# Reordered transfers, ScalarE copies and block transposes in a four-layer graph network on one Trainium2 core

## The chip, the core and the metric

The kernel runs on one core of a Trainium2 chip. A core has five engines that run side by side and meet only at semaphores: TensorE (matrix products, here PE), VectorE (DVE), ScalarE (ACT), GpSimd (POOL) and SyncE (SP). DMAs are issued from SP, ACT and POOL and are carried by 16 DMA engines that all queues share. The metric is the device time of one execution in microseconds (us), the median of several runs.

## What is computed

A graph of 3327 nodes with 512 features each goes through four layers. Every layer adds its result to its input and normalizes each row. Layers 0, 2 and 3 are graph attention with 8, 8 and 4 heads; layer 1 averages over up to 64 neighbours.

```python
def attention(h, adj, W, a):                      # layers 0 (no elu), 2 and 3
    Wh = h @ W                                    # by head
    e = leaky_relu(s1[:, None] + s2[None, :], 0.2)   # s1, s2: Wh times the two halves of a
    att = softmax(where(adj > 0, e, -9e15), axis=-1)
    return elu(att @ Wh)

def layer1(X, A):
    keep = (A > 0) & (cumsum(A, axis=1) <= 64)
    cnt = keep.sum(axis=1)
    xj = leaky_relu((keep @ X / max(cnt, 1)) @ W_nb.T + b_nb)
    return leaky_relu(X @ W_line.T + b_line) + where(cnt > 0, xj, 0)

x = layernorm(x + layer(x))                       # four times
```

## The kernel before

**Tiles and halves.** Nodes are cut into 26 tiles of 128 (`NT`), and these into two halves of 13 (`HALF`). The mask of edges stays in SBUF as 8-bit floats. An attention layer runs in eight units: for each half of the target nodes, four slices `s` of 128 features. With 8 heads a slice holds two heads (`HS == 2`, layers 0 and 2), with 4 heads one (`HS == 1`, layer 3).

**A unit** (`unit`, L361) loops over the 26 source tiles `j`. For each head, VectorE makes the weights `t` (L402) from a row broadcast `rb`, a column `qc` and the mask; ScalarE makes from `t` an 8-bit step `y` (L405); TensorE multiplies `t` with the values `vj` into `po` (L425). Two tiles later `den` (L377) adds the softmax denominators into `pd`, from `y` and from the small matrices `sden` and `sm`. These hold each source's factors, cut into three bf16 pieces whose sum is the factor, by `cut` (L321). For half 0 of the sources `cut` runs before the layer's loop, for half 1 as a job within its first unit.

**After a unit** `po` is copied to `ob` by ScalarE and VectorE, TensorE transposes it (L453), ScalarE copies the result to `hb` (L457; two buffers, `sp` pool) and SP stores it to the DRAM array `hd`. In layer 3, for half 0, the path is another (`by_dma`): VectorE transposes blocks of 32x32 straight out of `po` (L443) and four DMAs per unit place them in `hd` (L465). For half 1 of layer 3 (`final`) TensorE's transposes are taken into an SBUF array `g` instead of `hd` (L951 for the first two slices).

**Denominators.** When a half is done (in layer 3, half 1, after slice 1 and after slices 2 and 3) VectorE transposes `pd` into `db` (L486, L487) and sums the pieces into `red` (L491); SP writes these to a DRAM array `dd` in four DMAs (L495) and reads them back as `pes` (L498); `finish_sums` (L501) makes the reciprocals `rec`. For the very last slice TensorE does this with a product against `c1w` (L533).

**Order of work.** TensorE runs in the order of the program text. The other engines' orders are set by a scheduler from a model of the times, except where `keep_in_program_order` holds an instruction in its place. A job list spreads side work, one job for each source tile: `nothing` is an empty job. Each engine takes its instructions in that order, so one that waits holds back those behind it.

**Between the layers.** After layer 0, `finish` (L202) loads rows of `hd` and of the input (`xr`), divides by the denominators, adds and normalizes, two tiles at a time; the first two tiles are finished as `ending` of the last unit. Layer 1 (`sage`, L645) first projects each tile (L690, L693) into a value split in three bf16 parts, two kept in SBUF (`zs`) and one sent through DRAM (`zd`, read back as `zl`). Then, for each of 26 output tiles, TensorE adds 26 x 3 products into `acc` (L809). The kept edges `kt` (L774) are made beforehand by a running count in `pk`, which starts from carries `cy` that POOL loads for four source tiles at a time. `cb` and `cnt` (L740 to L745) are the neighbour counts of every node, `wsb` the weights of layer 2's projection, `bnb` a bias. Layer 2 is followed by `third` (L836), which finishes layer 2's tiles and projects them for layer 3.

## Time and profile before

| what | us |
|---|---|
| runs | 3405.98, 3407.31, 3412.4 |
| median | 3407.31 |
| profiled execution | 3407.9, span 3406.2 |

The span runs from the first to the last instruction that the profiler recorded. How it is shared out by stage, in us from its start:

| stretch | what runs |
|---|---|
| 0 to 145 | load of the mask, projection of layer 0 |
| 145 to 953 | attention of layer 0, with neighbour counts and the rest of the mask as jobs |
| 953 to 1005 | passage from layer 0 to layer 1 |
| 1005 to 1165 | layer 1, projections |
| 1165 to 1207 | layer 1, first output tile |
| 1207 to 1754 | layer 1, other output tiles, with layer 2's projection |
| 1754 to 1778 | passage to layer 2 |
| 1778 to 2556 | attention of layer 2 |
| 2556 to 2706 | passage and projection for layer 3 |
| 2706 to 3373 | attention of layer 3 |
| 3373 to 3406 | last slice, normalization and output |

Groups of instructions that the change touches, from the page and from the list of groups (count, busy us, mean ns of one):

| line, engine | what | count | busy | mean |
|---|---|---|---|---|
| L402 DVE | `t`, 128x1664 | 1040 | 1959.9 | 1957 |
| L405 ACT | `y`, 128x1664 | 1040 | 1771.1 | 1766 |
| L453 PE | transposes of `ob` | 260 | 44.7 | 290 |
| L486, L487 DVE | transposes of `pd` | 28 | 17.1 | 637, 586 |
| L491 DVE | sums of pieces | 14 | 6.9 | 530 |
| L348 DVE | `sm` from pieces | 20 | 6.8 | 380 |
| L629 DVE | counts to bf16, 128x512 | 6 | 4.1 | 683 |
| L635 DVE | `nb`, 128x512 | 6 | 4.1 | 681 |
| L951 DVE | `g` from PSUM, 128x512 | 6 | 4.1 | 683 |
| L533 PE | sums by product, last slice | 26 records | 3.1 | 257 |

A busy time is the union of a group's records, so groups of two engines may lie over each other. DMA issues on SP are not counted as busy: a slow issue shows only in the chain of waits and in SP's own order of instructions. Several short VectorE instructions in a row overlap by part of their length, so the distance between two starts is what one of them costs.

### The profile page before, as it was taken

How to read it: one execution, taken by the hardware profiler on the slowest of the kernel's cores; microseconds unless marked ns; L12 is line 12 of the kernel's file. 1: busy time of each engine (PE TensorE's matmuls, PEld its weight loads, DVE VectorE, ACT ScalarE, POOL GpSimd, SP SyncE). 2: the span in 40 equal slices, each digit the busy share in tenths (PEclk: the TensorE clock that was granted, in tenths of full speed). 3: DMA queues.
4: the chain of work that ended last, by engine and by line, in shares of the span. 5: the costliest groups of instructions: out<-in, count | busy, mean ns of one | idle time of the engine just before them, and what ended most of it. 6: DMA issues, size and time to landing. Idle time of an engine off the chain costs nothing.

```text
span 3406.2 us, 47019 instructions
## 1 busy us (share of the span) xinstructions
PE 3262.8 (96%) x18423; PEld 1631.0 (48%) x18423; DVE 2695.3 (79%) x2630; ACT 2351.4 (69%) x2128; POOL 214.7 (6%) x344
## 2 busy tenths in 40 slices
...
GB/s 372 214 127 123 52 49 53 42 49 28 38 123 128 116 111 87 90 85 85 85 81 26 41 50 48 56 44 47 35 25 225 169 41 42 41 51 79 95 42 48
DMA packets 313365, 284.65 MB, mean 84 GB/s; under 512 B 134253, under 2 KB 248631, under 8 KB 313144
## 3 DMA queue, kind: packets, MB, share of 16 engines
...
q8 instruction: 145, 2.38, 0.3%
...
## 4 chain that ended last, share of the span: by engine, by line
PE 79%; issue 7%; DVE 6%; DMA 4%; ACT 2%; POOL 0%; SPq 0%; ACTq 0%; POOLq 0%; DVEq 0%
PE po L425 49%; PE acc L809 9%; PE pd L377 7%; PE pw L268 5%; DVE t L402 4%; PE pz L690 3%; PE pi L693 3%; DMA raw<-in_adjT_dram 2%; ACT y L405 1%; PE pt L453 1%; DMA cy<-ctd 1%; PE pk L770 1%; PE pt L258 0%; PE pa L1022 0%; DVE mask L593 0%
## 5 line engine op out<-in xcount | busy, mean ns | idle before, releaser
L402 DVE SCALAR_TENSOR_TENSOR t<-rb,qc,mask 128x1664 f32<-128x1664 f32 x1040 | 1959.9, 1957 | 167.7 <-PE po L425 150.1
L405 ACT ACTIVATE y<-t,bi,sc 128x1664 fp8e4<-128x1664 f32 x1040 | 1771.1, 1766 | 317.3 <-PE pd L377 304.4
L425 PE MATMUL po<-t,vj 128*64 128x448 f32 (+3 forms) x8320 | 1924.6, 520 | 25.0 <-DVE t L402 22.3
L425 PEld LDWEIGHTS po<-t,vj 128*64 128x64 f32 (+1 forms) x8320 | 848.3, 148 | 978.2 <-issue 689.7
L809 PE MATMUL acc<-zs,kt 128*128 128x512 bf16 x1352 | 405.1, 382 | 0.0
L809 PEld LDWEIGHTS <-kt 128*128 128x128 fp8e4 x2028 | 199.1, 98 | 250.8 <-issue 9.5
L268 PE MATMUL pw<-wsb,xT 128*128 128x264 f32 (+1 forms) x1248 | 299.8, 395 | 9.2 <-DVE vt L274 7.5
L762 ACT CAST pk<-cy 128x512 f32<-128x512 bf16 x169 | 98.9, 587 | 294.5 <-DVE kt L774 251.1
L377 PE MATMUL pd<-y,sden 128*32 128x448 fp8e4 (+1 forms) x4160 | 259.4, 342 | 8.2 <-ACT y L405 8.2
L268 PEld LDWEIGHTS pw<-wsb,xT 128*128 128x128 f32 x1248 | 240.4, 196 | 53.4 <-issue 5.0
L809 PE MATMUL acc<-zl,kt 128*128 128x512 bf16 x676 | 257.8, 381 | 4.0 <-DMA zl<-zd 4.0
L774 DVE SCALAR_TENSOR_TENSOR kt<-pk,mask 128x512 fp8e4<-128x512 f32 x169 | 116.0, 687 | 99.7 <-PE pk L770 99.7
L377 PEld LDWEIGHTS <-sden 128*32 128x32 bf16 x4160 | 117.6, 96 | 160.3 <-issue 137.6
L274 DVE TENSOR_TENSOR vt<-pw,dc 128x256 f32<-128x256 f32 x156 | 59.0, 418 | 141.2 <-ACT dc L269 137.1
L356 POOL DMA_DIRECT2D rb<-r x40 | 21.9, 548 | 1617.0 <-DVE t L402 1604.5
L272 ACT COPY rc<-pw 128x8 f32<-128x8 f32 (+1 forms) x78 | 12.7, 163 | 138.7 <-PE pw L268 136.2
L690 PE MATMUL pz<-wn,xT 128*128 128x512 f32 x208 | 97.4, 613 | 10.1 <-ACT xT L684 10.1
L693 PE MATMUL pi<-wl,xT 128*128 128x512 f32 x208 | 93.5, 592 | 0.0
L659 POOL DMA_DIRECT2D cy<-ctd x91 | 67.9, 746 | 338.4 <-ACT pk L762 310.2
L782 DVE SCALAR_TENSOR_TENSOR y<-acc,cnt,bnb 128x512 f32<-128x512 f32 x26 | 19.5, 751 | 85.9 <-PE acc L809 85.9
L593 DVE TENSOR_SCALAR mask<-raw 128x832 fp8e4<-128x832 int32 (+2 forms) x90 | 53.1, 598 | 40.4 <-DMA raw<-in_adjT_dram 40.1
L154 ACT ACT_TABLE_LOAD x45 | 57.7, 1283 | 37.3 <-DVE mv L153 36.7
...
## 6 DMA issues: line engine op xcount, KB each, us to landing
...
```

What stands on the lines that cost most here:

```text
L268: nc.tensor.matmul(pw[e][:, :FW + H], xT[:, c, :], wsb[:, c, e, :], start=c == 0, stop=c == FC - 1)
L274: nc.vector.tensor_tensor(vt[:, hs, :], pw[e][:, :FW].rearrange("p (h d) -> p h d", d=D), self.dc[:, t, hs].rearrange("p (h e) -> p h e", e=1)
L377: nc.tensor.matmul(pd[c][32 * kk:32 * kk + 32, :w_], lhsT, rhs, start=(kk, c) not in seen, skip_group_check=final is not None, stop=last a ...
L402: nc.vector.scalar_tensor_tensor(t, rb[k], self.qc[:, j, h:h + 1], mask[:, j, i0:i0 + IW], op0=ALU.max, op1=ALU.mult)
L405: nc.scalar.activation(y, t, AF.Sigmoid, bias=self.bi[:, j, h:h + 1], scale=self.sc[:, j, h:h + 1], saturate=False)
L425: nc.tensor.matmul(po[c][k * D:(k + 1) * D, :z - a_], vj[:, j % 2, k * D:(k + 1) * D], ts[k][:, a_:z], start=j == 0, stop=j == NT - 1)
L659: nc.gpsimd.dma_start(out=cy[:, :n, :], in_=ctd[t:t + n, b * GW:(b + 1) * GW] .rearrange("(o t) i -> o t i", o=1).to_broadcast([P, n, GW]))
L690: nc.tensor.matmul(pz, xT[:, c, :], wn[:, c, :], start=c == 0, stop=c == FC - 1)
L693: nc.tensor.matmul(pi, xT[:, c, :], wl[:, c, :], start=c == 0, stop=c == FC - 1)
L762: nc.scalar.copy(pks[k % 2], carry[b, t // 4 * 4][:, t % 4:t % 4 + 2, :])
L774: nc.vector.scalar_tensor_tensor(kt, pk, NEIGHBOURS, mask[:, t:t + 2, i0:i0 + GW], op0=ALU.is_le, op1=ALU.mult, saturate=False)
L809: nc.tensor.matmul(acc, kts[t][:, s * P:(s + 1) * P], zs(t, c) if c < 2 else zl[:, t, :], start=t == 0 and c == 0, stop=t == NT - 1 and c ...
```

## The change

It has six parts.

1. `cut`: the six casts to bf16 pieces and the multiplications into `sm` run on ScalarE instead of VectorE.
2. `count_jobs`: the counts' cast runs on ScalarE, and `nb` is made from `ct` in SBUF instead of from `pn` in PSUM.
3. Denominators: for half 0 of layers 0 and 2 they are summed by TensorE (`by_pe`), with `pd` copied by ScalarE. Elsewhere, `dd` keeps the layout of `red`, is written with one DMA and read back by sixteen (`place`), on POOL, or on SP at the end of a layer (`end`), and there as the last job but one.
4. `finish` as `ending`: the two `xr` tiles lie in the two `hb` buffers, and in layer 2 `e` has two buffers.
5. Layer 1: `cb` and `cnt` move ahead of the projections; for the first output tile the `zl` products come after all others; `wsb` is loaded by SP after that tile instead of by POOL before it.
6. Layer 3, half 1, slices 0 and 1: block transposes and DMAs to `hd` as in half 0, and one DMA that reads `hd` back into `g` some jobs later.

The diff, cut to its core:

```diff
@@ -162,7 +162,7 @@
-    def finish_steps(pool, xin, layer, t0, n, hbufs=6, eng=nc.sync, xbufs=None):
+    def finish_steps(pool, xin, layer, t0, n, hbufs=6, eng=nc.sync, xbufs=None, xpool=None, ebufs=None):
         H, D = layer.H, layer.D
@@ -171,7 +171,8 @@
                 ys.append(h)
-                xr = pool.tile([P, F], F32, name="xr", bufs=xbufs)
+                xr = xpool.tile([P, F], F32, name="xr", tag="hb") if xpool else \
+                    pool.tile([P, F], F32, name="xr", bufs=xbufs)
                 load_tile(xr, xin, t, nc.gpsimd)
@@ -181,7 +182,7 @@
             if layer.elu:
-                e = pool.tile([P, F], F32, name="e")
+                e = pool.tile([P, F], F32, name="e", bufs=ebufs)
                 nc.scalar.activation(e, h, AF.Exp)
@@ -329,13 +330,13 @@
                     nc.vector.tensor_tensor(dc, dc, qc, op=ALU.mult)
-                ins = nc.vector.tensor_copy(pc[:, :, :, c0], dc)
+                ins = nc.scalar.copy(pc[:, :, :, c0], dc)
                 if pinned:
...
                 nc.vector.tensor_tensor(rest, dc, pc[:, :, :, c0], op=ALU.subtract)
-                nc.vector.tensor_copy(pc[:, :, :, c0 + 1], rest)
+                nc.scalar.copy(pc[:, :, :, c0 + 1], rest)
                 nc.vector.tensor_tensor(rest, rest, pc[:, :, :, c0 + 1], op=ALU.subtract)
-                nc.vector.tensor_copy(pc[:, :, :, c0 + 2], rest)
+                nc.scalar.copy(pc[:, :, :, c0 + 2], rest)
             HS = self.HS
@@ -345,8 +346,7 @@
                 for c0, f in ((0, -0.5), (3, -1.0)):
-                    nc.vector.tensor_scalar(m[:, :, :, c0:c0 + 3], pc[:, :, k::HS, c0:c0 + 3], f, None,
-                                            op0=ALU.mult)
+                    nc.scalar.mul(m[:, :, :, c0:c0 + 3], pc[:, :, k::HS, c0:c0 + 3], f)
@@ -432,11 +432,11 @@
             if ending:
-                ending()
+                ending(sp)
             den(NT - 2, late)
             ob = sp.tile([P, IW], F32, name="ob", bufs=1)
-            by_dma = HS == 1 and not final
+            by_dma = HS == 1 and not (final and s > 1)
             for c, (a_, z) in enumerate(CUTS):
@@ -465,6 +465,8 @@
                                       in_=ob[32 * b:32 * b + 32, :].rearrange("p (q f) -> p q f", f=32))
+                if final:
+                    jobs += [nothing] * 3 + [lambda: final(s, 0, HALF, None)]
             else:
@@ -479,7 +481,9 @@
                 nc.gpsimd.memset(db[64:, WB:], 0.0)
-            if not (final and s == NS - 1):
+            by_pe = HS == 2 and half == 0 or final and s == NS - 1
+            if not by_pe:
@@ -489,14 +493,20 @@
                     nc.vector.tensor_reduce(red[:, :, o, :], dv[:, :, :, 3 * o:3 * o + 3], AX.X, ALU.add)
-                dd = dram.tile([IW, 2, 2 * NS], F32, name=f"dd{self.li}{half}{s}")
-                for kk in range(4):
-                    i_, w_ = (0, WA) if kk < 2 else (WA, WB)
-                    nc.sync.dma_start(out=dd[i_:i_ + w_, kk % 2, :].rearrange("(b i) x -> i b x", i=32),
-                                      in_=red[32 * kk:32 * kk + 32, :w_ // 32].rearrange("p b o s -> p b (o s)"))
+                dd = dram.tile([P, WA // 32, 2 * NS], F32, name=f"dd{self.li}{half}{s}")
+                nc.sync.dma_start(out=dd, in_=red.rearrange("p b o s -> p b (o s)"))
                 pes = sp.tile([P, HALF, 2, 2, NS], F32, name="pes", tag="red", bufs=1)
-                nc.sync.dma_start(out=pes.rearrange("p q k o s -> p q (k o s)"),
-                                  in_=dd.rearrange("(q p) k x -> p q (k x)", p=P))
+                end = half == 1 and s == NS - 1
+                def place():
+                    for kk in range(4):
+                        q0, nq = (0, NA) if kk < 2 else (NA, HALF - NA)
+                        src = dd[32 * kk:32 * kk + 32, :4 * nq].rearrange("i (q m) x -> m i q x", m=4)
+                        for m in range(4):
+                            ins = (nc.sync if end else nc.gpsimd).dma_start(
+                                out=pes[32 * m:32 * m + 32, q0:q0 + nq, kk % 2].rearrange("p q o s -> p q (o s)"), in_=src[m])
+                            if end and kk + m == 0:
+                                tc.keep_in_program_order(ins)
@@ -512,33 +522,42 @@
-                jobs += [nothing] * max(0, 6 - len(jobs))
-                at = 6 if half == 0 or s < NS - 1 else len(jobs)
+                if end:
+                    return jobs + [place, finish_sums]
                 if final and s > 1:
-                    return [nothing] * 5 + [finish_sums] + jobs[2:]
-                return jobs[:at] + [finish_sums] + jobs[at:]
+                    return [nothing, nothing, place, nothing, nothing, nothing, finish_sums] + jobs[2:]
+                jobs += [nothing] * max(0, 7 - len(jobs))
+                return jobs[:2] + [place] + jobs[2:7] + [finish_sums] + jobs[7:]
...
                 nc.scalar.copy(db[:64, c * (WA // 2):(c + 1) * (WA // 2)], pd[c][:64, :WA // 2])
-                nc.vector.tensor_copy(db[64:, c * (WB // 2):(c + 1) * (WB // 2)], pd[c][64:, :WB // 2])
+                (nc.scalar.copy if HS == 2 else nc.vector.tensor_copy)(
+                    db[64:, c * (WB // 2):(c + 1) * (WB // 2)], pd[c][64:, :WB // 2])
             held = []
...
-                pe = po[0][:, :2 * HALF * H].rearrange("p (q o h) -> p q o h", q=HALF, o=2)
+                pe = po[0][:, :2 * HALF * H].rearrange("p (q o h) -> p q o h", q=HALF, o=2) if final else \
+                    qp.tile([P, HALF, 2, H], F32, name="pe", tag="q")
                 held.append(pe)
...
                     e = int(q >= NA)
-                    nc.tensor.matmul(pe[:, q, :, :], db[:, (q - e * NA) * P:(q - e * NA + 1) * P], c1w[:, :, e, :],
+                    cc = c1[:, :, 8 * e:8 * e + 8] if HS == 2 else c1w[:, :, e, :]
+                    nc.tensor.matmul(pe[:, q, :, :], db[:, (q - e * NA) * P:(q - e * NA + 1) * P], cc,
                                      start=True, stop=True)
             def reciprocals():
-                pe = held[0]
-                nc.vector.tensor_tensor(r_[:, :, 0, ss], pe[:, :, 0, ss], rc[:, :, 0, ss], op=ALU.mult)
-                nc.vector.tensor_tensor(r_[:, :, 0, ss], pe[:, :, 1, ss], r_[:, :, 0, ss], op=ALU.add)
+                pv = held[0].rearrange("p t o (k s) -> p t o k s", k=HS)
+                for k in range(HS):
+                    ins = nc.vector.tensor_tensor(r_[:, :, k, ss], pv[:, :, 0, k, ss], rc[:, :, k, ss], op=ALU.mult)
+                    if HS == 2:
+                        tc.keep_in_program_order(ins)
+                    nc.vector.tensor_tensor(r_[:, :, k, ss], pv[:, :, 1, k, ss], r_[:, :, k, ss], op=ALU.add)
                 nc.vector.reciprocal(rec[:, t0:t0 + HALF, hs], rec[:, t0:t0 + HALF, hs])
+            if not final:
+                return jobs[:2] + [sums, nothing, reciprocals] + jobs[2:]
@@ -626,13 +645,13 @@
                 ct = pool.tile([P, 4 * P], BF, name="ct", bufs=1)
-                nc.vector.tensor_copy(ct[:, :w_], held["p"][:, :w_])
+                nc.scalar.copy(ct[:, :w_], held["p"][:, :w_])
                 pn = qp.tile([P, 4 * P], F32, name="pn", tag="q")
...
                 nb = pool.tile([P, 4 * P], F8, name="nb", bufs=1)
-                nc.vector.tensor_scalar(nb[:, :w_], pn[:, :w_], 0.0, None, op0=ALU.is_equal, saturate=False)
+                nc.vector.tensor_scalar(nb[:, :w_], ct[:, :w_], 0.0, None, op0=ALU.is_equal, saturate=False)
                 nc.sync.dma_start(out=mask[P - 1:P, NT - 1, i0:i0 + w_], in_=nb[NT:NT + 1, :w_])
@@ -704,6 +723,14 @@
+                cb = zp.tile([P, NT], BF, name="cb")
+                nc.gpsimd.dma_start(out=cb, in_=ctd[NT:NT + 1, :].rearrange("o (t p) -> p (o t)", p=P))
+                cnt = zp.tile([P, 3, NT], F32, name="cnt")
+                nc.vector.tensor_scalar(cnt[:, 0, :], cb, NEIGHBOURS, 1.0, op0=ALU.min, op1=ALU.max)
+                nc.vector.reciprocal(cnt[:, 1, :], cnt[:, 0, :])
+                nc.vector.tensor_scalar(cnt[:, 2, :], cb, 0.0, None, op0=ALU.is_gt)
                 pend = None
@@ -727,8 +754,6 @@
                 wsb = wp.tile([P, FC, 2, FW + nxt.H], F32, name="wsb")
-                load_wide(wsb, wsrc, nc.gpsimd)
-                nc.vector.tensor_copy(wsb[:, :, :, FW:], wa[nxt.li].rearrange("p c (e h) -> p c e h", e=2))
@@ -736,13 +761,6 @@
                 nc.gpsimd.dma_start(out=bnb, in_=bn.to_broadcast([P, F]))
-                cb = wp.tile([P, NT], BF, name="cb")
-                nc.gpsimd.dma_start(out=cb, in_=ctd[NT:NT + 1, :].rearrange("o (t p) -> p (o t)", p=P))
-                cnt = wp.tile([P, 3, NT], F32, name="cnt")
-                nc.vector.tensor_scalar(cnt[:, 0, :], cb, NEIGHBOURS, 1.0, op0=ALU.min, op1=ALU.max)
-                nc.vector.reciprocal(cnt[:, 1, :], cnt[:, 0, :])
-                nc.vector.tensor_scalar(cnt[:, 2, :], cb, 0.0, None, op0=ALU.is_gt)
@@ -805,7 +823,8 @@
                                 kts += kept(0, len(kts))
-                            for c in range(3):
+                            for c in range(2 if t0 + s == 0 else 3):
                                 nc.tensor.matmul(acc, kts[t][:, s * P:(s + 1) * P],
@@ -815,6 +834,11 @@
                                 jobs.pop(0)()
+                        if t0 + s == 0:
+                            for t in range(NT):
+                                nc.tensor.matmul(acc, kts[t][:, :P], zl[:, t, :], start=False, stop=t == NT - 1)
+                            load_wide(wsb, wsrc, nc.sync)
+                            nc.vector.tensor_copy(wsb[:, :, :, FW:], wa[nxt.li].rearrange("p c (e h) -> p c e h", e=2))
                         y = output(acc, t0 + s)
@@ -948,7 +972,8 @@
                     if s < 2:
-                        nc.vector.tensor_copy(g[:, qs, s * P:(s + 1) * P], pt[:, :n])
+                        nc.gpsimd.dma_start(out=g[:, qs, s * P:(s + 1) * P], in_=hd[HALF * P:, s * P:(s + 1) * P]
+                                            .rearrange("(q p) f -> p q f", p=P))
                         return
@@ -1072,7 +1097,7 @@
         L0.attention(rp, first_jobs, mask_steps(rawp, pieces, 1, [k for k in range(len(pieces)) if k % 5 in (1, 3)], True),
-                     ending=lambda: ends.extend(finish(f0, x, L0, 0, 2, 2)))
+                     ending=lambda sp: ends.extend(finish(f0, x, L0, 0, 2, 2, nc.sync, None, sp)))
@@ -1088,7 +1113,7 @@
                              if (half, s) == (0, 0) else [],
-                             ending=lambda: ends.extend(finish(f2, x2, L2, 0, 2, 2)))
+                             ending=lambda sp: ends.extend(finish(f2, x2, L2, 0, 2, 2, nc.sync, None, sp, 2)))
             third(ends)
```

## The prediction

> **What bounds the kernel now.** I read three views in this order: the page's busy shares, busy time by stage, and the chain of waits inside two passages between stages. First the page:
>
> ```profile
> PE 3262.8 (96%) x18423; PEld 1631.0 (48%) x18423; DVE 2695.3 (79%) x2630; ACT 2351.4 (69%) x2128; POOL 214.7 (6%) x344
> ```
>
> TensorE looks like the bound at 96%. The stages say otherwise. In the next view the columns are the stretch and its length, then busy us of PE, PEld, DVE, ACT and POOL, the granted clock, the DMA share and GB/s:
>
> ```profile
> 145.00:952.90 807.90, 787.78 (x5724) 340.49 (x5726) 805.62 (x494) 736.18 (x490) 7.66 (x15) 0.99 0.20 60
> 952.90:1005.00 52.10, 36.48 (x153) 17.93 (x150) 29.31 (x65) 21.68 (x34) 9.46 (x16) 0.84 0.57 169
> 1165.00:1207.50 42.50, 32.60 (x111) 13.21 (x110) 14.73 (x25) 9.89 (x17) 10.10 (x13) 0.84 0.66 176
> 1778.50:2556.00 777.50, 768.41 (x5440) 348.29 (x5442) 777.39 (x444) 722.42 (x476) 7.07 (x14) 0.99 0.13 41
> 2556.00:2598.00 42.00, 22.31 (x136) 16.39 (x133) 26.72 (x58) 23.93 (x39) 11.85 (x19) 0.76 0.72 219
> 2706.00:3373.00 667.00, 664.07 (x2735) 333.37 (x2734) 488.25 (x416) 459.80 (x327) 17.28 (x31) 1.00 0.20 55
> ```
>
> The reader is to see three kinds of stage. In the attention of layers 0 and 2 (rows one and four) VectorE is busy 805.6 of 807.9 us and 777.4 of 777.5 us: it is the bound, and TensorE waits inside its rows. In layer 3 (last row) TensorE is the bound, 664 of 667 us. Rows two, three and five are passages: no engine is full, the clock is 0.76 to 0.84, the DMA share is 0.57 to 0.72. Here a chain of transfers decides. The chain of waits gives, for the passage after layer 0 and for the one inside layer 1 (start us, us, what):
>
> ```profile
> 964.56 6.68 SPq L495
> 971.30 3.01 SPq L495
> 974.35 2.84 DMA dd<-red
> 977.25 2.52 DMA pes<-dd
> 979.80 0.23 DVE rec L507
> ...
> 1179.26 11.53 DMA cb<-ctd
> 1190.81 0.18 DVE cnt L743
> 1191.26 0.64 DVE kt L774
> ```
>
> The first is the denominators' trip through DRAM, held up at the issue (L495) by full DMA engines. The second is a tiny load of counts, `cb`, for which VectorE waits in order, while `kt`, which feeds TensorE, stands behind it.
>
> **What the Trainium skill says.** "DMA: Bandwidth & Descriptors", section "Queues, rings and completion order": each DMA engine takes turns between the queues it has work for, packet by packet. The trace agrees that SP's small stores share the engines with POOL's loads: `hd<-hb` issued at 962.18 us frees its buffer for ScalarE only at 974.30, and an L495 issue that takes 0.54 us in mid-layer takes 6.68 here. "TensorE: Matmul & The Clock Gate", Part 1: an idle window of about 3.4 us puts the array back to half clock. The trace agrees: after 10.06 us idle, eight L690 records take 6.38 us, later 3.60. "VectorE: DVE Perf Modes", "Why PSUM operands drop a tier": SBUF sources allow faster modes than PSUM. No run here shows it for this operation. "ScalarE: Activation LUTs", "What ACT_TABLE_LOAD costs", is used below for a price.
>
> **The change part by part.** The sum is made against the profiled span, 3406.2 us; the median of the other runs is 3407.3, 1.1 above.
>
> Layers 0 and 2, in the loop. VectorE's cost of an operation is taken from start to start, since short ones overlap (a 0.40 us cast at 158.48 is followed by the next start 0.13 later).
> - Pieces to ScalarE: per cut, six casts (L332, L336, L338) and four multiplies (L348). Inside the loop of layer 0 they advance VectorE by 0.24 + 0.24 + 0.52 + 0.96 = 1.96 us, of layer 2 by 1.94. ScalarE gets six copies at 186 + 0.833 x 104 = 273 ns and four at 316 ns by the skill's price, an estimate of 2.9 us, within its 72 us idle in row one and 55 us in row four. The added wait: each subtraction (L335, L337) now waits for a ScalarE copy queued among sigmoids of 1.77 us, and the `t` operations behind it on VectorE, so TensorE, wait with it. Between 0 (other `t` are ordered in between) and 4.7 us each (ScalarE's longest such wait for `pd`). I take 0, as VectorE has six `t` buffers.
> - Half-0 denominators: four transposes 2.46, two reduces 0.90, four products 0.48 and a reciprocal 0.71 = 4.55 us leave VectorE; four products 0.48 and a reciprocal 0.71 come back. Saved 3.35 us a layer. TensorE gets 13 products, 26 records, 3.07 us by the same group in the tail (L533). Four copies of `pd` go to ScalarE, 4 x 0.5 = 2 us. The four dd writes and one read-back vanish here.
> - Counts (layer 0 alone): eight casts L629, 4.05 us, move to ScalarE (8 x 0.57, from the 128x512 copy L457). L635, 3.98 us in all, reads SBUF instead of PSUM: 0 to 3 saved, I take 2. The wait added: the product L631 stands in TensorE's order 2.4 us behind its cast, and may now wait up to one sigmoid, 1.77 us.
>
> So VectorE loses 1.96 + 3.35 + 4.05 + 2 = 11.4 us in layer 0 and 1.94 + 3.35 = 5.3 in layer 2. TensorE is close behind: 16 products take 3.01 us when they do not wait, plus 0.87 / 2 of `pd`, 3.44 us per source tile against 3.73 paced by VectorE. After the other products about 4 us a unit of room is left, so the lead is used up slowly. I take 70%: **-8.0 and -3.7 us**; bounds 0 and the whole.
>
> Layer 3, first two heads of half 1. Four groups of transposes (0.60 + 0.60 + 0.66 + 0.33 = 2.19 us) leave TensorE twice: 4.4 us where it is the bound. VectorE swaps a 0.61 copy and 2.3 of L951 copies for four block transposes, 2.10 us, within its idle time. ScalarE loses six copies. Eight L465 stores on SP (4.6 us for four) lie between prefetched `vj` loads, as after half 0, where TensorE shows no gap; two read-backs and three sets of sixteen small loads go to POOL, busy 17 of 667 us. Against it, VectorE's transposes must free `po` in time: 0 to 2 us. **-4**, from -8 (the 1.78 us wait and slow clock at 3209 go too) to +1.
>
> Passage inside layer 1. `cb` and its three operations move ahead of the first loop, `wsb` (1 MB) behind the first output tile, and that tile's `zl` products to its end. Now the first tile runs 1176 to 1207.4, 31 us; at full rate it needs 78 x 0.216 + 13 x 0.216 = 19.7. What remains is carries `cy`: five loads, two buffers, each some 4 to 5 us to land while `zl` streams, bring the last pair to about 1194; then its products and 26 x 0.216 = 5.6 us of `zl` end near 1200. **-7** (-10 to -3). `wsb` is needed some 25 us later and hidden; its two issues stand behind the `zl` loads on SP.
>
> Passage to layer 2. The cut of half 0 shares VectorE with the first `t`: from 1769.29 to 1772.77 it holds them back 3.5 us, and TensorE's 2.39 us wait at 1778.5 is for such a `t`. Half of the cut goes: **-1.5** (-3 to +2, if copies queue behind L292's 2.98 us DMA wait).
>
> Passage after layer 2. The second `xr` load, now with its own buffer, no longer waits for the first sum (issued at 2562.98, landed 2566.2), nor `e`; TensorE's first gap, 10.61 us, shrinks, but the second, 8.85 us, waits for tiles behind `rec`. The path to `rec`: one dd write (instead of 8.1 us of L495), the last `hd` store at about 2570.1, then sixteen small reads on SP. SP's issues here cost 0.33 to 0.67; at 0.5 that is 8 us, landing 1.9 later: 2580.5 against 2583.3. **-3** (-10 to +3).
>
> Passage after layer 0. The same, but here the last `hd` stores wait for ScalarE, 976.0. Then 8 us of issues and 1.9: `rec` at 986 instead of 979.8. The four `h` loads on SP (977.7) wait behind them too. `cb` on POOL (1.49 us to issue, some 3 us of crawling DMA at 1187) comes between `blb` and the `h` loads. The paired `xr` saves VectorE 2.29 us that are not on the path. **+5** (-6, if tiles 2 and 3 go ahead of `rec`, to +10).
>
> Sum: -8.0 - 3.7 - 4 - 7 - 1.5 - 3 + 5 = -22.2 us, 0.65%: 3407.3 - 22.2 = **3385 us**.
>
> **The rivals.**
> - A, all of it lands: VectorE's whole 16.7, layer 3 -8, passages -10, -3, -10, -6: -54, 3354 us. For it: VectorE has no idle time. Against: TensorE is 2% behind.
> - B, the passages give it back: the sixteen pieces issue at 1 us each, as L495 does when engines are full. Passage after layer 0 +13, after layer 2 +5, the rest as forecast: -24.2 + 18 = -6, 3401 us.
> - C, slower: VectorE waits for ScalarE at each piece. Twelve handovers in two in-loop cuts at 4.7 us are +56, less the -22: 3441 us. It decides once a handover costs over 22.2 / 12 = 1.9 us, about one sigmoid. For it: ScalarE is 91% busy and takes its queue in order. Against: many `t` can stand between the subtractions.
>
> That the change is not what runs is excluded: each part changes instructions.
>
> **How the numbers follow.** Forecast 0.52 (3372 to 3396), A 0.16, B 0.20 (3396 to 3407), C 0.12. A measurement of this kernel tells 0.2%, 6.8 us, from no change. Faster than 3400.5: 0.52 + 0.16 + 0.13 of B = 0.81; within: 0.07 of B and 0.02 of C = 0.09; slower: 0.10. The range 3360 to 3405 leaves out part of A, a little of B and C.
>
> **What would show it.** Right: no VectorE wait on `cb` near 1190, the first output tile near 22 us, layers 0 and 2 shorter by some 8 and 4 us at VectorE 100%, layer 3 shorter by 4. Wrong: VectorE idle before L335 or L337, TensorE idle before L631, `rec` after layer 0 later than 990, or a layer 3 no shorter.

## The result, and the profile after

| kernel | median us | runs | lowest to highest | ratio to before, 95% interval |
|---|---|---|---|---|
| before | 3406.99 | 4 | 3405.98 to 3412.4 | |
| changed | 3421.33 | 4 | 3418.32 to 3425.04 | 1.0039 (1.0022 to 1.0057) |
| changed, again beside later runs | 3420.81 | 10 | 3415.31 to 3423.4 | 1.0030 (1.0020 to 1.0039) |

The change makes the kernel slower by 0.3 to 0.4%, 11 to 14 us. The forecast was 22 us faster, and 3421 lies outside its range of 3360 to 3405. The profiled execution has a span of 3420.7 us against 3406.2 before.

The page of the changed kernel, busy time of each engine:

```profile
PE 3258.0 (95%) x18397; PEld 1625.6 (48%) x18449; DVE 2671.0 (78%) x2552; ACT 2377.1 (69%) x2196; POOL 242.4 (7%) x392
```

VectorE did lose 24 us of work (2695.3 before), and ScalarE took on 26. Read alone, this line says that the change did what it was made for. The stages say otherwise. Below are busy times by stretch of the changed kernel, with the same columns as in the prediction; the stretches answer to its six rows in order of time, and the seventh row is the first of layer 0's eight units:

```profile
149.10:957.20 808.10, 785.89 (x5750) 336.31 (x5752) 795.03 (x470) 743.59 (x512) 8.98 (x17) 0.99 0.20 60
957.20:1016.00 58.80, 34.75 (x153) 18.09 (x149) 30.06 (x68) 24.54 (x37) 9.64 (x15) 0.80 0.52 144
1186.80:1218.00 31.20, 23.85 (x89) 9.73 (x90) 7.80 (x12) 6.43 (x12) 5.77 (x8) 0.84 0.79 223
1786.00:2566.00 780.00, 768.08 (x5470) 347.54 (x5472) 776.92 (x435) 733.17 (x494) 9.15 (x18) 0.99 0.13 41
2566.00:2610.00 44.00, 27.88 (x159) 20.52 (x156) 30.81 (x70) 28.11 (x44) 12.39 (x20) 0.81 0.67 219
2714.00:3387.00 673.00, 664.03 (x2709) 331.32 (x2708) 484.68 (x406) 459.77 (x329) 47.65 (x81) 0.99 0.22 60
149.10:274.10 125.00, 111.69 (x811) 45.96 (x811) 114.63 (x88) 106.90 (x86) 1.12 (x2) 0.93 0.37 110
```

In layer 0's loop VectorE is now idle for 13 us of 808 (2.3 us of 807.9 before), and 10.4 of these lie in the first unit alone (last row: 114.63 busy of 125.00). In layer 3 TensorE, the bound there, is idle for 9 us where it was idle for 3, and POOL is busy 48 us instead of 17.

To see where the time went, I cut both spans at TensorE's products: the first and last `po` product of each layer, the start of each of its eight units, the first `pz` of the third projected tile (the first that needs `rec`), and the first `acc` product of output tiles one and two.

| stage, us | before | changed | changed again | forecast | measured, first profile |
|---|---|---|---|---|---|
| start to first `po` | 145.0 | 149.1 | 149.0 | not counted | +4.1 |
| layer 0, units 1 to 8 | 811.6 | 811.8 | 808.5 | -8.0 | +0.2 |
| of it: unit 1 | 120.0 | 125.0 | 121.8 | | +5.0 |
| unit 3 (counts) | 102.4 | 99.8 | 99.8 | | -2.6 |
| unit 5 (denominators) | 100.8 | 97.9 | 97.9 | | -2.9 |
| passage after layer 0 | 41.0 | 47.6 | 49.0 | +5 | +6.6 |
| layer 1, first output tile | 31.3 | 31.2 | 30.5 | -7 | -0.1 |
| passage to layer 2 | 21.3 | 22.2 | 22.8 | -1.5 | +0.9 |
| layer 2, units 1 to 8 | 784.8 | 783.4 | 783.6 | -3.7 | -1.4 |
| of it: unit 1 | 105.0 | 107.1 | 107.4 | | +2.1 |
| unit 5 (denominators) | 101.4 | 98.0 | 98.0 | | -3.4 |
| passage after layer 2 | 146.0 | 144.3 | 145.0 | -3 | -1.7 |
| layer 3, units 1 to 8 | 669.1 | 675.0 | 674.7 | -4 | +5.9 |
| of it: units 6, 7, 8 | 84.8, 84.3, 81.4 | 82.7, 90.9, 82.8 | 82.7, 90.6, 82.8 | | -2.1, +6.6, +1.4 |

The measured column sums to +14.5, the difference of the spans; the stages left out moved by 0.5 or less. The rows of whole layers are sums of the eight rounded units. Most units whose work is the same repeat to 0.1 us from profile to profile. Some stages don't: the start and layer 0's first unit, where VectorE waits for the mask's loads, the passages after layers 0 and 2, and unit 5 of layer 0, which took 97.9, 98.9 or 100.5 in kernels with the same part 3. Kernels that run the same instructions there differ by 2 to 7 us, so only larger differences, or ones that several kernels show, are read from them.

Part of this spread goes with TensorE's granted clock (the third number from the end of a row). Unit 5 of layer 0 in the changed kernel and in two of the kernels below:

```profile
575.68:673.55 97.87, 96.88 (x729) 43.04 (x727) 97.37 (x57) 92.55 (x65) 1.26 (x3) 1.00 0.16 50
```

```profile
562.66:661.50 98.84, 97.85 (x729) 44.07 (x727) 97.62 (x57) 92.55 (x65) 1.26 (x3) 0.98 0.16 50
```

```profile
567.03:667.54 100.51, 99.52 (x730) 44.76 (x728) 97.65 (x57) 92.55 (x65) 1.26 (x3) 0.97 0.15 49
```

VectorE's and ScalarE's work is the same to 0.3 us, and the unit is longer as the clock is lower: 97.9 at 1.00, 98.8 to 98.9 at 0.98, 100.5 at 0.97 in all kernels with part 3. Where two units are compared below, the clock of both matters.

Four places in the trace of the changed kernel carry the rest. The first is before layer 0's loop, in order of time (start, us, engine, line, what; in brackets the idle time before it and what ended it):

```profile
85.09 0.82 ACT L333 CAST pc<-dc 128x104 bf16<-128x104 f32 x1
85.42 1.39 ACT L312 COPY rr<-pr 8x512 f32<-8x512 f32 x2
86.39 1.23 PE L310 MATMUL pr<-ident,rc 128*8 128x128 f32 x5 [5.37 <-ACT rr L312]
```

`rr`, which empties the PSUM bank that TensorE's next transposes need, now stands behind the casts of `pc` in ScalarE's order, and these wait for VectorE's subtractions. TensorE waits 5.37 us; before, 0.51.

The second is layer 0's first unit:

```profile
173.60 1.95 DVE L402 SCALAR_TENSOR_TENSOR t<-rb,qc,mask 128x1664 f32<-128x1664 f32 x1 [3.44 <-PE po L425]
...
176.46 0.24 ACT L312 COPY rr<-pr 8x128 f32<-8x128 f32 x1
...
176.61 0.66 ACT L333 CAST pc<-dc 128x104 bf16<-128x104 f32 x1
...
186.42 0.55 ACT L648 CAST ct<-pct 128x512 bf16<-128x512 f32 x1
...
187.03 0.58 PE L650 MATMUL pn<-ct,below 128*128 128x512 bf16 x1 [3.53 <-ACT ct L648]
...
193.44 1.95 DVE L402 SCALAR_TENSOR_TENSOR t<-rb,qc,mask 128x1664 f32<-128x1664 f32 x1 [3.08 <-PE po L425]
```

The first cast of `cut` comes at 176.61, right behind the last of four `rr` copies, two of which wait for the transfer of the one before. Counted from the layer's first product that is 14 us later than in the kernel before, where it ran on VectorE (at 158.48). There the cut filled VectorE's time up to 170; now VectorE makes six `t` in a row, has no free buffer left and is idle for 3.44 us. The cut comes when it is short of time again, and meets the counts: their cast `ct` queues behind the pieces and the sigmoids, TensorE waits 3.53 us for it, and VectorE runs out of free buffers once more (3.08).

The third is the passage after layer 0, from the chain of waits:

```profile
968.42 10.94 DMA hd<-hb
979.45 0.54 ACT hb L457
...
981.07 0.61 SPq L506
...
981.74 5.85 DMA pes<-dd
...
988.47 1.65 DMA pes<-dd
...
990.25 0.21 DVE rec L517
990.46 0.60 DVE st L152
...
991.52 0.57 ACT xT L703
992.13 5.26 PE pz L709 x8
```

`rec` is there at 990.25, which is 29.5 us after the layer's last product (960.8); before, 23.3. The sixteen reads are issued only from 981.07 on, since SP takes its queue in order and the second pair of `hd` stores stands ahead of them. The chain goes on behind `rec`: VectorE has the statistics `st` of the next pair there, a root on ScalarE waits for these, and ScalarE's copy `xT` of the first tile stands behind that root, although this tile needs no `rec`. TensorE's first projection starts 31.3 us after the layer's last product, 19.1 before. From `rec` on the passage then takes 18.2 us, 17.7 before, so nearly all of the 6.6 us lies ahead of `rec`.

The fourth is the end of unit 7 in layer 3:

```profile
3300.60 1.28 ACT L962 ACT_TABLE_LOAD   x1
3301.89 0.42 ACT L962 ACTIVATE e<-g 128x256 f32<-128x256 f32 x1
3302.32 1.28 ACT L405 ACT_TABLE_LOAD   x1
3303.62 1.77 ACT L405 ACTIVATE y<-t,bi,sc 128x1664 fp8e4<-128x1664 f32 x1
...
3305.44 0.91 PE L377 MATMUL pd<-y,sden 128*32 128x448 fp8e4 x6 [4.46 <-ACT y L405]
```

An exponential for `g` with its two table loads, 3 us in all, stands in front of the unit's last sigmoid. The unit can't end without that one, and TensorE waits 4.46 us.

### The profile page after: what moved, and what is told of

The parts are those of the page before. It is cut to its first block, busy times and chain, and to the rows that moved or that the text cites. A ratio compares the mean times of both kernels' runs of the same rounds, so it can differ in the third digit from the quotient of the medians.

```text
span 3420.7 us, 47075 instructions
## 1 busy us (share of the span) xinstructions
PE 3258.0 (95%) x18397; PEld 1625.6 (48%) x18449; DVE 2671.0 (78%) x2552; ACT 2377.1 (69%) x2196; POOL 242.4 (7%) x392
## 4 chain that ended last, share of the span: by engine, by line
PE 80%; issue 6%; DMA 5%; ACT 4%; DVE 4%; POOL 1%; SPq 0%; ACTq 0%; POOLq 0%; DVEq 0%
PE po L425 49%; PE acc L828 10%; PE pd L377 7%; PE pw L269 5%; DVE t L402 3%; PE pz L709 3%; PE pi L712 3%; DMA raw<-in_adjT_dram 2%; ACT y L405 2%; DMA cy<-ctd 1%; PE pt L453 1%; PE pk L788 1%; DMA hd<-hb 0%; PE pa L1047 0%; PE pt L259 0%
## 5 line engine op out<-in xcount | busy, mean ns | idle before, releaser
L425 PEld LDWEIGHTS po<-t,vj 128*64 128x64 f32 (+1 forms) x8320 | 838.4, 148 | 986.1 <-issue 708.9
L828 PE MATMUL acc<-zs,kt 128*128 128x512 bf16 x1312 | 394.5, 382 | 2.2 <-issue 0.2
L828 PE MATMUL acc<-zl,kt 128*128 128x512 bf16 x638 | 241.8, 379 | 0.6
L356 POOL DMA_DIRECT2D rb<-r x40 | 21.3, 532 | 1692.9 <-DVE t L402 1667.8
```

The source lines that it names most:

```text
L425: nc.tensor.matmul(po[c][k * D:(k + 1) * D, :z - a_], vj[:, j % 2, k * D:(k + 1) * D], ts[k][:, a_:z], start=j == 0, stop=j == NT - 1)
L828: nc.tensor.matmul(acc, kts[t][:, s * P:(s + 1) * P], zs(t, c) if c < 2 else zl[:, t, :], start=t == 0 and c == 0, stop=t == NT - 1 and c ...
```

## The experiments

Stages of all kernels that ran, in us (profiled execution), then span, median of all runs and ratio. u is a unit, p0, p1 and p2 are the passages after layer 0, to layer 2 and after layer 2, o1 the first output tile.

| kernel | start | L0 u1 | L0 u3 | L0 u5 | p0 | o1 | p1 | L2 u1 | p2 | L3 u6 | u7 | u8 | span | median | ratio (95%) |
|---|---|---|---|---|---|---|---|---|---|---|---|---|---|---|---|
| before | 145.0 | 120.0 | 102.4 | 100.8 | 41.0 | 31.3 | 21.3 | 105.0 | 146.0 | 84.8 | 84.3 | 81.4 | 3406.2 | 3407.0 | |
| changed | 149.1 | 125.0 | 99.8 | 97.9 | 47.6 | 31.2 | 22.2 | 107.1 | 144.3 | 82.7 | 90.9 | 82.8 | 3420.7 | 3421.3 | 1.0039 (1.0022, 1.0057) |
| b0_changed_again | 149.0 | 121.8 | 99.8 | 97.9 | 49.0 | 30.5 | 22.8 | 107.4 | 145.0 | 82.7 | 90.6 | 82.8 | 3420.3 | 3420.8 | 1.0030 (1.0020, 1.0039) |
| a1_cut_vector | 144.6 | 116.4 | 99.8 | 98.8 | 47.5 | 30.6 | 23.7 | 105.4 | 146.1 | 82.7 | 89.2 | 82.9 | 3409.0 | 3413.6 | 1.0015 (1.0008, 1.0022) |
| c2_cut_alone | 149.6 | 121.9 | 102.4 | 100.8 | 40.7 | 31.9 | 22.9 | 105.4 | 146.2 | 84.8 | 84.3 | 81.4 | 3415.0 | 3416.9 | 1.0028 (1.0019, 1.0038) |
| c4_pin_on_vector | 148.1 | 117.3 | 99.8 | 100.5 | 48.2 | 31.0 | 22.6 | 107.3 | 144.9 | 82.7 | 90.7 | 82.7 | 3416.4 | 3414.4 | 1.0018 (1.0010, 1.0026) |
| a2_counts_vector | 149.2 | 124.6 | 102.4 | 97.9 | 47.1 | 30.9 | 22.2 | 107.1 | 147.5 | 82.7 | 90.9 | 82.9 | 3426.9 | 3426.2 | 1.0046 (1.0029, 1.0063) |
| a4_pe_layer3 | 148.6 | 122.5 | 99.8 | 97.9 | 47.1 | 30.7 | 21.5 | 105.6 | 143.9 | 84.8 | 82.5 | 81.2 | 3407.5 | 3412.6 | 1.0009 (1.0000, 1.0017) |
| c1_slots_later | 148.3 | 121.8 | 99.8 | 97.9 | 47.2 | 31.3 | 21.7 | 105.6 | 145.2 | 82.7 | 83.6 | 81.2 | 3408.6 | 3411.8 | 1.0014 (1.0005, 1.0022) |
| a3_dd_old | 146.5 | 120.3 | 99.8 | 98.9 | 46.9 | 30.8 | 22.7 | 107.4 | 144.1 | 82.7 | 87.2 | 81.4 | 3407.7 | 3409.5 | 1.0005 (0.9997, 1.0014) |
| b1_old_ending_layer0 | 148.9 | 122.6 | 99.8 | 98.9 | 47.8 | 30.6 | 22.7 | 107.3 | 145.7 | 82.7 | 89.2 | 83.1 | 3420.6 | 3420.1 | 1.0029 (1.0018, 1.0040) |
| b2_layer1_old | 148.7 | 122.8 | 99.8 | 98.9 | 48.1 | 31.4 | 21.7 | 106.7 | 146.0 | 82.7 | 89.2 | 82.9 | 3420.2 | 3424.9 | 1.0043 (1.0029, 1.0057) |
| d1_zl_between | 147.3 | 120.8 | 99.8 | 97.9 | 47.7 | 28.9 | 22.8 | 107.4 | 148.9 | 82.7 | 90.9 | 82.4 | 3419.2 | 3421.9 | 1.0036 (1.0023, 1.0050) |
| d4_third_carry | 147.4 | 123.3 | 99.8 | 98.9 | 54.5 | 27.5 | 22.7 | 107.3 | 150.5 | 82.7 | 89.2 | 82.4 | 3426.9 | 3424.6 | 1.0043 (1.0030, 1.0057) |
| b3_best | 144.5 | 117.2 | 99.8 | 98.8 | 44.4 | 30.4 | 23.1 | 105.4 | 143.2 | 85.0 | 82.5 | 81.2 | 3397.1 | 3398.2 | 0.9968 (0.9956, 0.9979) |
| c3_best_layer1_old | 143.6 | 116.7 | 99.8 | 97.9 | 40.7 | 31.8 | 22.5 | 105.0 | 143.3 | 84.9 | 82.5 | 81.2 | 3391.4 | 3397.8 | 0.9969 (0.9958, 0.9981) |
| d2_sixteen_reads | 145.3 | 116.6 | 99.8 | 100.5 | 48.4 | 31.5 | 21.9 | 105.0 | 146.7 | 85.5 | 83.9 | 81.2 | 3410.2 | 3408.5 | 0.9998 (0.9990, 1.0006) |
| d3_best_zl_slots | 145.6 | 116.7 | 99.8 | 97.9 | 41.3 | 28.7 | 23.9 | 105.4 | 140.6 | 82.7 | 83.6 | 81.2 | 3390.1 | 3398.2 | 0.9965 (0.9952, 0.9977) |

Each ratio is to runs of the kernel before on the same chip and in the same hour, whose medians were 3407.0 to 3409.4; compare ratios rather than medians across rows.

### The pieces on ScalarE

**a1_cut_vector** takes part 1 out of the changed kernel:

```diff
-                ins = nc.scalar.copy(pc[:, :, :, c0], dc)
+                ins = nc.vector.tensor_copy(pc[:, :, :, c0], dc)
...
-                nc.scalar.copy(pc[:, :, :, c0 + 1], rest)
+                nc.vector.tensor_copy(pc[:, :, :, c0 + 1], rest)
...
-                nc.scalar.copy(pc[:, :, :, c0 + 2], rest)
+                nc.vector.tensor_copy(pc[:, :, :, c0 + 2], rest)
...
-                    nc.scalar.mul(m[:, :, :, c0:c0 + 3], pc[:, :, k::HS, c0:c0 + 3], f)
+                    nc.vector.tensor_scalar(m[:, :, :, c0:c0 + 3], pc[:, :, k::HS, c0:c0 + 3], f, None,
+                                            op0=ALU.mult)
```

> The changed kernel with the six casts and four multiplies of cut (part 1) back on VectorE, all else as changed. Theory (ScalarE as a link in the chain of cut is what costs): the first po product comes 4 us earlier again (145 instead of 149), the first unit of layer 0 takes 121 instead of 125.0, the passage to layer 2 21.3 instead of 22.3, the first unit of layer 2 105 instead of 107.1; the sum is 11 us, 3410 instead of 3421. Rival (the first unit of layer 0 is slow because of the counts' cast on ScalarE): that unit stays at 124 to 125, the sum is 7 us or less, 3414. Forecast's own view (the move to ScalarE saves): slower by 2 to 4 us, 3424.

Measured: 1.0015 against 1.0030 and 1.0039, so some 5 to 8 us of the loss are part 1's. The start is back at 144.6. Unit 1 of layer 0 is at 116.4, below the 120.0 of before, and VectorE is full there again. The first of the next two rows is unit 1 in the kernel before, the second is unit 1 in a1:

```profile
145.00:265.00 120.00, 109.61 (x811) 46.84 (x811) 119.33 (x102) 102.50 (x72) 1.12 (x2) 0.96 0.38 114
```

```profile
144.60:261.00 116.40, 108.04 (x809) 45.70 (x809) 116.18 (x98) 103.78 (x76) 1.12 (x2) 0.96 0.39 118
```

VectorE has 1.6 us more work than in the changed kernel (116.18 against 114.63) and the unit is 5 to 9 us shorter. Five kernels of the table have the pieces on VectorE and the counts on ScalarE (a1, b3, c3, d2, d3): start and unit 1 together take 260.3 to 262.3 in them. The nine with both on ScalarE, c4 aside, take 266.8 to 274.1. The means are 261.4 and 270.5, so the move costs 9 us there, part of it together with a lower granted clock in unit 1 (0.96 in the five, 0.93 to 0.96 in the nine). Layer 0's units sum to 804.2, 7.4 us less than before, and layer 2's to 781.7, 3.1 less: what was forecast for the two loops (8.0 and 3.7, of which 1.4 each was the pieces') is nearly all there, once the pieces are back on VectorE. The passage to layer 2 did not get shorter (23.7, expected 21.3).

**c2_cut_alone** is the same part put alone into the kernel before (the diff of a1 read the other way).

> The kernel before with part 1 alone: the six casts and four multiplies of cut on ScalarE. Theory (ScalarE as a link in that chain costs by itself): first po product at 149 instead of 145.0, first unit of layer 0 124 instead of 120.0, of layer 2 107 instead of 105.0; 3419. Rival (the first unit suffers only together with the counts' cast, which queues behind the pieces): 149, 120, 107; 3415. Forecast's view: 3405.

Measured: 1.0028, so this part is harmful without the others. The start is 149.6, as both expected. Unit 1 of layer 0 takes 121.9, between the two expectations; with the start it makes 271.5 against 265.0 before, 6.5 us. The other kernel with the pieces on ScalarE and the counts on VectorE, a2 below, takes 273.8 for the two. So 6.5 to 8.8 of the 9 us above come without the counts' cast, and its meeting with the pieces explains little of them. Unit 1 of layer 2 is 105.4, no slower than before: of the 2 us there in the changed kernel, no part is shown to come from the pieces. (That unit sits at 107 in nine kernels with the pieces on ScalarE and at 105.4 to 105.6 in three others, two of which (a4, c1) differ from the changed kernel only in layer 3. The granted clock of the unit is 0.94 in the nine and 0.95 to 0.97 in the three. What brings the lower clock stays open.)

**c4_pin_on_vector** leaves the pieces on ScalarE and moves only the mark that keeps the first of them in program order:

```diff
-                ins = nc.scalar.copy(pc[:, :, :, c0], dc)
+                nc.scalar.copy(pc[:, :, :, c0], dc)
+                ins = nc.vector.tensor_tensor(rest, dc, pc[:, :, :, c0], op=ALU.subtract)
                 if pinned:
                     tc.keep_in_program_order(ins)
-                nc.vector.tensor_tensor(rest, dc, pc[:, :, :, c0], op=ALU.subtract)
```

> The changed kernel with the pin of cut moved from ScalarE's first copy to VectorE's first subtraction. Theory (the pin holds the first copy behind four rr copies that wait for transfers, so the chain starts 18 us later and meets the counts): first unit of layer 0 117 to 118 instead of 122 to 125, of layer 2 105.5 instead of 107.2, start as changed, 149; 3413. Rival (each handover between the engines costs in itself, wherever it stands): 122 or more and 107; 3421.

Measured: unit 1 takes 117.3, as the theory had it. Its row:

```profile
148.10:265.40 117.30, 107.02 (x809) 45.60 (x809) 114.22 (x88) 107.91 (x85) 1.12 (x2) 0.96 0.39 118
```

VectorE's and ScalarE's work is that of the changed kernel to about 1 us, and the unit is 3 to 8 us shorter than in the nine kernels with the old mark (120.3 to 125.0). The two of these with the same granted clock of 0.96 take 120.3 and 120.8, so 3.0 to 3.5 us are the order's own; the others have 0.93 or 0.94. So in this unit it is the place of the chain in ScalarE's order that cost, not the handovers: the pieces now go ahead of and between the `rr` copies. The start (148.1) and layer 2 (107.3) are not touched by it, as expected for the first and not for the second.

### The counts

**a2_counts_vector** takes part 2 out of the changed kernel: `ct` is cast by VectorE and `nb` reads `pn`.

> The changed kernel with the counts' cast and the operand of nb (part 2) back as before, all else as changed. Theory (cut is the cause in the first unit, the counts alone help): the first unit of layer 0 stays within 1 us of 125.0, its third unit, which has counts only, goes from 99.8 back to 102.4; 3423 to 3424. Rival (the counts' cast on ScalarE makes the first unit slow): first unit 121 or less, third 102.4; 3419.

Measured: unit 3, where the counts are alone, goes back to 102.4 exactly, and unit 1 stays at 124.6. The counts help by 2.6 us where nothing collides; 1.0046 is in line with it, though its interval overlaps that of the changed kernel.

### The passage after layer 0

Three kernels each undo one part that touches it. **a3_dd_old** has four `dd` writes and one read, everywhere:

```diff
-                dd = dram.tile([P, WA // 32, 2 * NS], F32, name=f"dd{self.li}{half}{s}")
-                nc.sync.dma_start(out=dd, in_=red.rearrange("p b o s -> p b (o s)"))
+                dd = dram.tile([IW, 2, 2 * NS], F32, name=f"dd{self.li}{half}{s}")
+                for kk in range(4):
+                    i_, w_ = (0, WA) if kk < 2 else (WA, WB)
+                    nc.sync.dma_start(out=dd[i_:i_ + w_, kk % 2, :].rearrange("(b i) x -> i b x", i=32),
+                                      in_=red[32 * kk:32 * kk + 32, :w_ // 32].rearrange("p b o s -> p b (o s)"))
...
+                nc.sync.dma_start(out=pes.rearrange("p q k o s -> p q (k o s)"),
+                                  in_=dd.rearrange("(q p) k x -> p q (k x)", p=P))
```

> The changed kernel with the old layout of dd: four writes and one read on SP in place of one write and sixteen reads; the sums by TensorE for half 0 stay. Theory (the sixteen reads cost): from the last po of layer 0 to the second pair of projections 42 to 44 us instead of 47.6 (41.0 before), and the third unit of layer 3's second half shorter by 2 or more of its 90.9, since rec is there earlier; 3414. Rival (in the passage the sqrt table load in front of the last sigmoid and the hd stores cost, not the reads; in layer 3 the block transposes cost): passage 47 to 48, that unit 90 to 91; 3420.

**b1_old_ending_layer0** has the old `finish` as `ending` of layer 0, and nothing else undone:

```diff
-                     ending=lambda sp: ends.extend(finish(f0, x, L0, 0, 2, 2, nc.sync, None, sp)))
+                     ending=lambda sp: ends.extend(finish(f0, x, L0, 0, 2, 2)))
```

> The changed kernel with part 4 undone in layer 0 alone: the second xr load of the two tiles finished in the last unit waits for the first sum again. Theory (the early xr lets the square root of the norm run ahead of the last sigmoid, two table loads of 1.28 us and 0.29 in front of it): TensorE's wait before the last pd products falls from 3.08 to about 1, and the passage after layer 0 takes 44.5 instead of 47.6; 3418. Rival (the reads on SP and the cb load on POOL set the passage alone): 47 to 47.6; 3421.

**b2_layer1_old** undoes part 5 (`cb`, `cnt`, `wsb` and `zl` as before).

> The changed kernel with part 5 undone: cb, cnt, wsb and the zl products as before. Forecast's view (the part saves 7 us in the first output tile): that tile as before, 31.3 with all else worse by 0, so 3421 since the changed kernel shows 31.2 too, or 38 if the part does save 7 and something else lost it, 3428. Theory (the part gains nothing: the waits for cb go, and the 26 zl products that came between now follow at the end): first tile 31 to 32, passage after layer 0 1 us shorter without the cb load on POOL, passage to layer 2 1 us shorter; 3419.

Measured: 46.9, 47.8 and 48.1, against 47.6 and 49.0 of the changed kernel. None of the three gives the passage back by itself. In b1 the mechanism was as expected, but nothing of it reaches the passage's end; its timeline shows the wait gone (3.08 in the changed kernel) and the square root behind the last sigmoid:

```profile
960.94 1.77 ACT L405 ACTIVATE y<-t,bi,sc 128x1664 fp8e4<-128x1664 f32 x1 [0.77 <-PE pd L377]
962.73 1.28 ACT L154 ACT_TABLE_LOAD   x1
962.76 0.54 PE L377 MATMUL pd<-y,sden 128*32 128x448 fp8e4 x6 [0.93 <-ACT y L405]
```

`rec` comes 27.0 us after the layer's last product, 29.4 in the changed kernel. But ScalarE now has the root and both normalized tiles of the next pair ahead of `xT`, so that TensorE's first projection starts at 30.1 instead of 31.3, and from `rec` on 20.8 us pass instead of 18.2.

a3 is nevertheless the best of the single repairs, at 1.0005. Of the 13 us between its profile and the changed kernel's, 5 lie in layer 3 (units 7 and 8 at 87.2 and 81.4, as its theory had it), and 7 in the start and unit 1 of layer 0, where both run the same instructions in the same order, so that I don't count these as its doing. But the median of its 12 runs is 9 to 12 us better too, more than the 5 us of layer 3; where the rest comes from stays open.

**c3_best_layer1_old** undoes all three together, and parts 1 and 6 with them; it is **b3_best** (told below) without part 5.

> The better kernel (b3) with part 5 undone too. Theory (cb on POOL within the passage after layer 0 delays the loads behind it): that passage 41 to 42 instead of 44.4, first output tile 31.3 instead of 30.4, passage to layer 2 21.5 instead of 23.1; 3394 to 3395. Rival (part 5 is neutral, the passage varies by its transfers): 44, 3398.

The passage is 40.7, what it was before. b3, which keeps part 5 and with it the `cb` load on POOL in front of the loads of `h`, has 44.4: that load is worth some 3 to 4 us here (d3, which has it in the middle of the projections, shows 41.3). In total the two kernels are equal, 0.9968 and 0.9969.

**d2_sixteen_reads** then puts the one write and sixteen reads alone back into c3.

> The better kernel c3 with one dd write and sixteen reads at the end of layers 0 and 2 instead of four writes and one read, nothing else. Forecast's step (the reads' issues on SP make the passage after layer 0 five us longer by themselves): 45 to 46 instead of 40.7; 3402. Rival (the passage is held by several chains of like length, hd stores, reads, cb, so that one alone costs or gives back little): 41 to 42, passage after layer 2 within 1 of 143.3; 3398.

Measured: 48.4 instead of 40.7, 146.7 instead of 143.3 after layer 2, and 3408.5 instead of 3397.8. The medians differ by 10.7 us, as the two passages together (11.1). The forecast's own step is right, then: the reads cost 7.7 us by themselves (forecast 5). `rec` comes 27.9 us after the layer's last product, 22.8 in c3, so 5.1 of the 7.7 lie ahead of it. The rest lies behind, where TensorE's first projection starts at 31.0 instead of 18.4 us, since `xT` stands behind the next pair's root as in the changed kernel; this share is read from the timelines and not tested by itself. SP's issues in d2, in order of time:

```profile
956.84 1.31 SPq L459 DMA_DIRECT2D hd<-hb  x2
958.94 0.33 SPq L496 DMA_DIRECT2D dd<-red  x1
969.39 0.91 SPq L459 DMA_DIRECT2D hd<-hb  x2
970.39 9.17 SPq L505 DMA_DIRECT2D pes<-dd  x16
979.66 1.81 SPq L126 DMA_DIRECT2D h<-hd  x4
```

The same in c3:

```profile
953.33 0.97 SPq L459 DMA_DIRECT2D hd<-hb  x2
955.42 10.03 SPq L501 DMA_DIRECT2D dd<-red  x4
965.55 1.02 SPq L459 DMA_DIRECT2D hd<-hb  x2
967.94 0.36 SPq L507 DMA_DIRECT2D pes<-dd  x1
968.40 2.11 SPq L126 DMA_DIRECT2D h<-hd  x4
```

In c3 the four slow writes, 10.03 us of issues, run while the second `hd` pair has to wait in any case for the first to land; behind that pair comes one read. In d2 SP has nothing to do between 959.3 and 969.4, and the sixteen reads, 9.17 us, come behind the pair, where nothing covers them. In the changed kernel several things hold this passage at about 47 us, the reads, the late `hd` landing and the load of `cb`, so taking out any one of them showed next to nothing.

### Layer 3

**a4_pe_layer3** undoes part 6: TensorE's transposes and VectorE's copies into `g`.

```diff
-            by_dma = HS == 1 and not (final and s > 1)
+            by_dma = HS == 1 and not final
...
-                if final:
-                    jobs += [nothing] * 3 + [lambda: final(s, 0, HALF, None)]
...
-                        nc.gpsimd.dma_start(out=g[:, qs, s * P:(s + 1) * P], in_=hd[HALF * P:, s * P:(s + 1) * P]
-                                            .rearrange("(q p) f -> p q f", p=P))
+                        nc.vector.tensor_copy(g[:, qs, s * P:(s + 1) * P], pt[:, :n])
```

> The changed kernel with TensorE's transposes for the first two slices of layer 3's second half (part 6 undone), all else as changed. Theory (block transposes on VectorE and the late read-back of g push the jobs of the next unit to its end): layer 3's units 6, 7 and 8 go from 82.7, 90.9, 82.8 to 84.8, 85, 82; 3415. Rival (the sixteen reads on POOL push rec and the jobs, part 6 saves TensorE 4.4 us as forecast): units 84.8, 92, 83; 3424.

Measured: units 84.8, 82.5, 81.2, together 248.5 against 256.4 changed and 250.5 before. The rival falls: sixteen reads on POOL without part 6 are no loss here. Part 6 costs 7.9 us as it stands, although TensorE's 2.1 us do leave unit 6 (82.7 instead of 84.8). What it changes for the unit after is when `rec` is there. In us from the start of unit 7, `rec` is made at 17.1 before, 24.8 in a4 and 40.7 in the changed kernel (30.7 in a3, which has part 6 but not the sixteen reads), and the last exponential of the first two slices starts at 71.3, 63.7 and 86.5, with the unit's end at 84.3, 82.5 and 90.9.

**c1_slots_later** keeps part 6 and everything else, and puts ten empty jobs ahead of the last four groups of these jobs:

```diff
                         for q0 in range(0, HALF, 2):
+                            if q0 == 6:
+                                jobs += [none] * 10
                             jobs += first_slots(q0, min(2, HALF - q0))
                     else:
-                        jobs += [none] * 12
                         jobs += [lambda q=q: nc.vector.bn_stats(out=st[:, q, 0, :], in_=g[:, q, :FB])
```

> The changed kernel with the last four groups of layer 3's first two slices (divide, exponential, add) moved ten source tiles on, into the last unit, and the statistics' twelve empty jobs there dropped. Theory (rec comes late behind the read-back of g, so the exponentials, each with two table loads, stand in front of the last sigmoids of unit 7, where TensorE waits 4.46 us): unit 7 of layer 3 takes 86 instead of 90.7, unit 8 at most 1 us more than 82.8; 3416. Rival (the burst on VectorE at the unit's start, four transposes of po and four of pd ahead of the next t, is what costs): unit 7 stays at 90 or more; 3420.

Measured: units 82.7, 83.6, 81.2, together 247.5, and 1.0014 in all. `rec` is nearly as late as before the move (39.0), and the two waits at the unit's start, 0.96 and 2.09 us, are still there. Of the four exponentials only the last is in unit 8, beside others of its table. The first three stay in unit 7, at 69.7, 70.3 and 76.9 us from its start, and the first two of them share their table loads: unit 7 has 16 such loads instead of 20. So the exponentials have left the end of unit 7, where ScalarE now runs its sigmoids back to back and the last `pd` products have no gap:

```profile
3294.24 1.26 ACT L445 COPY ob<-po 128x448 f32<-128x448 f32 x3
3294.74 0.94 PE L377 MATMUL pd<-y,sden 128*32 128x448 fp8e4 x16
...
3295.39 5.11 ACT L405 ACTIVATE y<-t,bi,sc 128x1664 fp8e4<-128x1664 f32 x3
```

So these exponentials and their table loads, as they stood, cost 7 us in unit 7 and 1.6 in unit 8. With them put right, layer 3 is at 666.1, 3.0 us below before. But a4, without part 6, is at 667.1, so only 1.0 of these are part 6's: TensorE's 2.1 us leave unit 6, and unit 7 takes 83.6 against 82.5 in a4.

### The first output tile

b2 (above) has shown that part 5 as a whole makes no difference to this tile: 31.4 without it, 30.5 to 31.2 with it. Its last `kt`, counted from the tile's first product, comes at 27.7 in b2 and 27.6 before, and at 22.7 in the changed kernel. The wait for `cb` is gone, 5 us of it. But the tile ends 8.5 us after that `kt` (3.7 before), since all the `zl` products now follow:

```profile
1198.39 0.58 PE L788 MATMUL pk<-mask,upto 128*128 128x512 fp8e4 x1 [4.27 <-ACT pk L780]
...
1211.98 5.78 PE L839 MATMUL acc<-zl,kt 128*128 128x512 bf16 x26
...
1217.60 0.59 PE L828 MATMUL acc<-zs,kt 128*128 128x512 bf16 x2
```

**d1_zl_between** puts these products back between the others and keeps the early `cb` and the late `wsb`:

```diff
-                            for c in range(2 if t0 + s == 0 else 3):
+                            for c in range(3):
...
-                            for t in range(NT):
-                                nc.tensor.matmul(acc, kts[t][:, :P], zl[:, t, :], start=False, stop=t == NT - 1)
```

> The changed kernel with the zl products of the first output tile in their old places; cb and cnt stay early, wsb stays late. Theory (the tile is paced by the carries cy, its last kt comes 22.7 us after its start, and the 26 zl products put behind it add 5.8 us that had lain in its waits before): first tile 25 to 27 instead of 30.5 to 31.2; 3416. Rival (the zl products then wait for zl's transfers, which is why they were put last): 30 to 31; 3421.

Measured: 28.9, between the two. TensorE now waits for `zl` at the start, and only once:

```profile
1188.37 0.58 PE L828 MATMUL acc<-zl,kt 128*128 128x512 bf16 x1 [6.45 <-DMA zl<-zd]
```

Putting them last does avoid that wait, as it was meant to, and costs more at the end. The whole kernel is not faster for the 2 us (1.0036).

**d4_third_carry** adds a third buffer for the carries to d1 and loads one more ahead:

```diff
-                tc.tile_pool(name="sg_c", bufs=2, reuse_waits="tile") as cyp:
+                tc.tile_pool(name="sg_c", bufs=3, reuse_waits="tile") as cyp:
...
             load_carry()
+            load_carry()
```

> The d1 kernel with a third buffer for the carries cy and one more of them loaded ahead. Theory (the carries pace the first output tile, each load landing 4 us after an issue that waits for a cast): 22 to 24 us instead of 25 to 27. Rival (TensorE's clock and the zl transfers set it): as d1.

Measured: 27.5, so a third buffer is worth 1.4 us, and the theory's 22 to 24 falls. The wait for `zl` at the start is as long as in d1 (6.46 us). The added load sits in the passage after layer 0, which becomes 54.5, 7 us longer: one more load on POOL there costs more than it gives. (The profiled execution was the slowest of four, and the medians of d4 and d1 differ by only 2.7 us.)

### Putting the repairs together

**b3_best** has the pieces on VectorE, TensorE's transposes in layer 3, the old `ending` of layer 0, and four writes and one read at the ends of layers 0 and 2. It keeps the counts on ScalarE, the sums by TensorE, the sixteen reads within layer 3, part 5 and layer 2's `ending`.

> The changed kernel with what cost taken out: cut on VectorE, TensorE's transposes in layer 3's second half, the old ending of layer 0, and at the end of layers 0 and 2 four dd writes and one read; the counts on ScalarE, the sums by TensorE, the sixteen reads within layer 3, part 5 and layer 2's ending stay. Theory (the parts add up by stage): 3408.6 less 3.6 and 2.6 (counts), 2.9 and 3.4 (sums by TensorE), 2.0 (layer 3) and 1.5 (passage after layer 2), 3392 to 3394. Rival (gains of one stage are given back in the next, as the order of the other engines is set anew): 3402 or more.

**d3_best_zl_slots** keeps the block transposes with the jobs moved as in c1, loads `cb` in the middle of the projections, and has `zl` between.

> Cut on VectorE, old ending of layer 0, old dd at the ends of layers 0 and 2 (as in b3), with layer 3's block transposes and the slots moved on as in c1, cb loaded in the middle of the projections, zl between. Theory (all by stage): passage after layer 0 41, first output tile 26, layer 3's units 6 to 8 82.7, 83.6, 81.2; 3391. Rival (the tile stays at 31 and layer 3 gives back): 3398.

Measured: 0.9968 and 0.9965, 3398.2 us both. By stage d3 shows what was expected in the passage (41.3) and in layer 3 (82.7, 83.6, 81.2), not in the first output tile (28.7, expected 26). Its profiled span is 7 us shorter than b3's, but the medians agree; these kernels' runs spread over 5 to 9 us, and none of b3, c3 and d3 can be told from the others. All three are faster than both kernels, by 0.3% than before and by 0.6 to 0.7% than the changed one.

**b0_changed_again** is the changed kernel unaltered; its numbers stand in the tables above.

> The changed kernel as it is, beside the others of this call, since the stretch to the end of layer 0's first unit took 274.1, 273.8, 266.8 and 271.1 us in four kernels that have the same order of instructions there. Expected: 3417 to 3422, that stretch 266 to 274; the other stages within 0.5 us of the first profile (passage after layer 0 47.6, third unit of layer 3's second half 90.9).

## Why the prediction was wrong

- **Pieces in the loop: "I take 0, as VectorE has six `t` buffers".** This step failed, in layer 0. The waits at the subtractions themselves are small (0.2 to 1.0 us), so the buffers do what I said. What I didn't ask is where in ScalarE's order the first copy would stand: behind four `rr` copies (it is pinned there), 14 us later than on VectorE. The trace suggests why that matters: the casts had cost VectorE little before, as without them it runs out of buffers, and later they meet the counts. c4 shows that it matters: same engines, other place, 117.3 instead of 120 to 125. The price of a piece was low too, though ScalarE had room for it: I had 273 ns for a copy and 2.9 us for a cut, and the copies take 0.64 us and the cut of unit 1 keeps ScalarE busy for 4.8 us.
- **Pieces before the loop: not costed at all.** I costed the half-0 cut of layer 2 (-1.5) and forgot the same cut of layer 0, which runs in the middle of the projections. It costs 4 us there, alone (c2: 149.6) and with the rest. ScalarE's copies `rr`, `rc` and `xT` free PSUM for TensorE at each step of that stage, and I never looked at whom the pieces would hold up.
- **Denominators and counts: right.** Units 5 of layers 0 and 2 are 2.9 and 3.4 us shorter (3.35 a layer times 0.7 forecast; 0.3 to 2.9 and 1.7 to 3.5 over all kernels with part 3, the low ends at a granted clock of 0.97), unit 3 by 2.6 in every kernel with the counts on ScalarE. `nb` takes 0.42 us from SBUF where it took 0.68 from PSUM, 1.6 us for the six full ones where I took 2. With the pieces back on VectorE the loops give -7.4 and -3.1, where the forecast without its share for the pieces is -6.6 and -2.3.
- **Layer 3, -4, measured +5.9.** TensorE's two groups of transposes do leave. The failed step is to have counted the read-back of `g` and the loads on POOL as free because POOL is idle: what counts is that `rec` comes 24 us later (40.7 against 17.1), so that jobs with table loads run into the unit's end. c1 gives -3.0 with the jobs moved, of which 1.0 is part 6's.
- **First output tile, -7, measured about 0.** "then its products and 26 x 0.216 = 5.6 us of `zl` end near 1200", 24 us after the tile's start, failed in its first half. The mis-sized term is the carries: I had five loads at 4 to 5 us each and the last pair at 18 us. Those five took 5.7 to 9.1 us from issue to landing, the last `kt` came at 22.7, and the tile's end at 31.2. The 5.8 us of `zl` are as worked out; before, they lay in waits and cost nothing.
- **Passage after layer 0, +5, measured +6.6 to +8.0.** Right, and for the reason given: `rec` at 990.25 less the 4.1 us by which the layer ended later is 986, the time forecast; d2 gives 7.7 for the reads alone, 5.1 of it ahead of `rec`. That the projections of the first two tiles, which need no `rec`, would stand behind it was not foreseen. What a3 adds is that one can't find this by undoing it in the changed kernel, where other chains end at the same time.
- **Passages to and after layer 2: -1.5 and -3, measured +0.9 and -1.7.** The first isn't there in any kernel of the table; the second is within the 141 to 150 that this stage spans. With all else equal, the sixteen reads cost 3.4 there (d2).
- **The rivals.** C was on the right side and named the right engine, VectorE waiting on ScalarE; its price, up to 4.7 us at each of twelve handovers, wasn't what happened. The loss comes at two places, before the loop and in one unit, together 9 us. B's mechanism, reads that issue one by one, is real, but at 0.6 us each (forecast B: 1 us) and mainly in one passage. Of the forecast's own signs of error three came: TensorE idle before the counts' product (3.53 us), `rec` later than 990 (990.25) and a layer 3 no shorter. No rival had them together.

The sum moves from -22.2 to +14.5, 36.7 apart: layer 3 9.9, layer 0's loop 8.2, the output tile 6.9, the start 4.1, layer 2's loop 2.3, the passage to layer 2 2.4, the passage after layer 0 1.6, the passage after layer 2 1.3.
